# Order of softmax passes, top-k rounds and attention steps in a four-layer gated Flamingo kernel

## The chip, the cores and the metric

The kernel runs on one NeuronCore of a Trainium2 chip. A core has five engines that matter here, each with its own instruction queue: TensorE (PE, matmuls and transposes; its weight loads are listed as PEld), VectorE (DVE), ScalarE (ACT), GpSimd (POOL) and SyncE (SP, which issues most DMAs). They work side by side and wait for each other by semaphores. Matmul results land in PSUM, which this kernel hands out in eight banks of 512 floats a partition; everything else lies in SBUF.

The metric is the device time of one execution in microseconds. Times shown are medians of repeated runs; the profile is of one execution.

## What is computed

`x` is 4 x 256 tokens of 256 features, `ctx` 4 x 256 tokens of 64 features. Four layers follow each other, each with a cross attention and a feed-forward part, both added through a gate:

```python
x = x + jnp.tanh(g_xattn[0]) * _L0_xattn_ref(_layernorm(x), ctx, W_k, b_k, ln_gamma, ln_beta)
x = x + jnp.tanh(g_ffn[0])   * _L0_ffn_ref(_layernorm(x), gate_w, gate_b, expert_w, expert_b)
x = x + jnp.tanh(g_xattn[1]) * _L1_xattn_ref(_layernorm(x), ctx, Wq, Wkv_expand, Wout)
x = x + jnp.tanh(g_ffn[1])   * _L1_ffn_ref(_layernorm(x), w_gate, w_up, w_down)
x = x + jnp.tanh(g_xattn[2]) * _L2_xattn_ref(ctx, _layernorm(x), Wq, Wk, gamma_raw)
x = x + jnp.tanh(g_ffn[2])   * _L2_ffn_ref(_layernorm(x), w12, w3, router_w, expert_bias, sw1, sw2, sw3)
x = x + jnp.tanh(g_xattn[3]) * _L3_xattn_ref(_layernorm(x), ctx, ctx)
x = x + jnp.tanh(g_ffn[3])   * _L3_ffn_ref(_layernorm(x), W_router, W_sgate, Ws_gate_up, Ws_down, We_gate_up, We_down)
```

The change concerns the first third. Of it, the parts that matter:

```python
def _L0_xattn_ref(p, k_v, W_k, b_k, ln_gamma, ln_beta):      # p: the normalised x
    kv = k_v @ W_k.T + b_k
    sim = jnp.einsum('bid,bjd->bij', jnp.einsum('bij,bjd->bid', p, kv), kv) * 256 ** -0.5
    sim = (sim - mean(sim)) * rsqrt(var(sim) + EPS) * ln_gamma + ln_beta
    return softmax(sim)

def _L0_ffn_ref(x, gate_w, gate_b, expert_w, expert_b):      # 8 experts, all computed
    _, top_idx = jax.lax.top_k(x @ gate_w + gate_b, 2)
    all_out = relu(jnp.einsum('nsd,edo->nseo', x, expert_w) + expert_b)
    return jnp.take_along_axis(all_out, top_idx[..., None], axis=2).mean(axis=2)

def _L1_xattn_ref(q, latent_kv, Wq, Wkv_expand, Wout):       # 16 heads of 16, causal
    ...
    attn = softmax(where(tril, q k^T / 4, -max));  out = attn @ v
    return out @ Wout.T

def weight_quant(w):                                         # in L1's feed-forward part
    scale = 1.0 / clip(mean(abs(w)), EPS)
    return clip(round(w * scale), -1, 1) / scale

def _L2_xattn_ref(h, adj_raw, Wq, Wk, gamma_raw):            # a graph over the 256 context tokens
    sim = einsum('bhnd,bhmd->bnm', Q, K) / (4 * 4)
    threshold = top_k(sim, 76)[0][:, :, -1:]
    A = sigmoid(sim) * (sim >= threshold)
    A = (A + swapaxes(A)) * 0.5
    gamma = sigmoid(gamma_raw)
    return (1 - gamma) * adj_raw + gamma * A                 # adj_raw: the normalised x
```

The graph of layer 2 and the ternary weights of layer 1 depend on the context and the weights alone. The kernel therefore computes them early, in gaps of the layers before.

## The kernel before

The 1024 tokens are eight tiles of 128 partitions (two halves of four tiles). The stretch that the change touches is written in one function and ends when the attention of layer 1 ends, at about 258 us of the span. It has three stages.

**Prologue** (to about 54 us). `layernorm(h)` (L169 to L188) normalises the four tiles of a half: statistics on DVE (L176, L177), `ln_ve` (L179), a power on POOL (L181, `ln_rstd`), then four scalings to `xn` on DVE (L185). `transposed` (L190) turns four tiles by PE and copies the result out of PSUM to `xnT` by `evac`, which alternates between DVE (L109) and ACT (L111). Layer 0's attention then goes half by half: `similarities` (L616) turns the tiles, multiplies by the values (L623), copies `oT` on ACT (L628), forms the similarities twice, raw and scaled by gamma (L633), and squares the first on ACT (L641). `softmax0` (L647) computes the variance term on DVE (`s0_ve`, L650), its power on POOL (L652), the scaled similarities and maxima on DVE, and the exponentials on ACT (L666). `add0` (L671) adds the result to `x`. In between stand the key side (`kvmean` L609, `keys` L613 and L614) and the graph's projections and scores (`graph_projections` L462, `graph_scores` L472, copied into `gsim`). A bias block at L447 to L456 splits the expert biases into three bf16 parts on DVE and sends them through DRAM into `eb`, by SP.

**Dense stage** (to about 122 us). `route` (L206) and `choose` (L737) pick two of eight experts for each token. `dense` (L748) computes all eight for a tile: a bias matmul from `eb` (L752), 16 matmuls (L758) into four banks, relus with the chosen weights as scale on ACT (L766), pair sums on POOL (L771, L772). Tiles 0 to 5 run in a loop (L783 to L811), which also holds:

- *rounds of the graph's top-76*. Eight tiles need ten rounds each, 80 in all. A round is a MAX8 (L490) and a MATCH_REPLACE8 (L493) on a row of 256; the tenth has a comparison (L497) instead of the replacement. `graph_rows(n)` issues the next n rounds. The loop asks for 3 + (2, 3, 4, 4, 1, 2)[t], 34 in all.
- `keys1` and `values1` for layer 1 (L527, L542), and the second half's `transposed` and `route`.
- *ternary weights*: `ternary_mean(n)` takes the sum of magnitudes on ACT (two passes, L561), reduces it over partitions on PE (L565) and forms scale and reciprocal on DVE (L567 to L569); `ternary_scale` scales on ACT (L573) and clips on DVE (L574); `ternary_round` finishes on ACT (L578).

**Attention of layer 1** (to about 258 us). `Maxima(b)` (L843) projects the queries of batch b (L204); its `score(j)` makes masked scores of four heads (masks L837, scores L863 and L868) only to find row maxima on DVE (L874, four reductions, then `cm` L879 and L880); `late(j)` turns these (L886) and adds them to the queries on DVE (L889). `Sums(b)` scores again with the maxima subtracted (L903, L908), exponentiates on ACT (L914), multiplies by the values (L922, L927) and divides on DVE (L946, L948). A loop of 24 steps and five more (L978 to L1017) runs them: step n takes head group j = n % 4 of batch n // 4, with the sums one batch behind the maxima. Steps 0 and 1 also hold dense tiles 6 and 7, step 2 the third ternary weight. Each step ends with a call for three rounds.

What sets the order: inside `in_order` a queue keeps the order of the code. PE is in hand order throughout. ACT and DVE are in hand order up to the end of the dense loop, where `all_orders.close()` ends it; from there a scheduler may move their instructions among each other. POOL and SP are always left to the scheduler; the order that it finds is fixed in the built program.

Of the kernel before, what the change touches and what calls it, by code (L numbers as in the profile page):

```python
# [65 lines left out]
def flamingo(ctx: ExitStack, tc: tile.TileContext, a: dict, out: bass.AP):  # L66
# [97 lines left out]
    nc.gpsimd.memset(ones, 1.0)  # L164
    neghalf = const.tile([P, HT], F32, tag="neghalf", name="neghalf")
# [281 lines left out]
    eb_parts = tc.dram_tile([3, E * D], BF16, name="eb_parts")  # L447
    for n in range(3):
        eb_n = const.tile([16, P], BF16, tag=f"eb_{n}", name=f"eb_{n}")
        nc.vector.tensor_copy(eb_n, ebias)  # L450
        if n < 2:
            nc.vector.tensor_sub(ebias, ebias, eb_n)
        nc.sync.dma_start(eb_parts[n].rearrange("(p f) -> p f", p=16), eb_n)
    eb = const.tile([P, 2 * D], BF16, tag="eb", name="eb")
    for j in range(E // 2):
        nc.sync.dma_start(eb[32 * j : 32 * j + 3, :], eb_parts[:, j * 2 * D : (j + 1) * 2 * D])  # L456

# [98 lines left out]
    def ternary_mean(n):  # L558
        wsum = sm([2], "w_sum")
        for j in range(2):  # L560
            nc.scalar.activation(  # L561
                wq1[n][:, j * FF1 : (j + 1) * FF1], raw[n][j], AF.Abs, accum_out=wsum[:, j : j + 1]
            )
        pw = bank()[:, :2]
        nc.tensor.matmul(pw, ones, wsum, start=True, stop=True)  # L565
        m, r = mw[:, n : n + 1], rmw[:, n : n + 1]
        nc.vector.tensor_reduce(m, pw, AX.X, ALU.add)  # L567
        nc.vector.tensor_scalar(m, m, 1.0 / (FF1 * D), 1e-5, ALU.mult, ALU.max)
        nc.vector.reciprocal(r, m)  # L569
# [6 lines left out]
    def ternary_round(n):  # L576
        for j, w in enumerate(raw[n]):
            nc.scalar.activation(wq1[n][:, j * FF1 : (j + 1) * FF1], w, AF.Copy, bias=-ROUND)  # L578

# [7 lines left out]
    with tc.tile_pool(name="l0a", bufs=1) as lp:  # L587
# [15 lines left out]
        for i in range(2):  # L603
            nc.vector.tensor_tensor(
                kvn[:, :, i], pn[i].rearrange("p (h j) c -> p h j c", h=2),
                bk[:, :C].unsqueeze(1).unsqueeze(1).to_broadcast([P, 2, 2, C]), ALU.add,
            )
        mean = lp.tile([P, 2], F32, tag="kvmean", name="kvmean")
# [7 lines left out]
        def similarities(h, tiles):  # L616


            xt = transposed(tiles)
# [8 lines left out]
            nc.scalar.copy(oT, po)  # L628
            sims = [[bank().rearrange("p (i s) -> p i s", i=2) for _ in range(2)] for _ in range(2)]
# [15 lines left out]
            return sims[1], square  # L645

        def softmax0(h, pss, square):  # L647

# [3 lines left out]
            nc.gpsimd.tensor_tensor(rstd, ve, neghalf, ALU.pow)  # L652
            nc.vector.tensor_scalar_mul(rstd, rstd, 1.0 / 16.0)
# [3 lines left out]
            for i in range(HT):  # L657
# [3 lines left out]
                if i % 2:  # L661
# [3 lines left out]
                    for k in (i - 1, i):  # L665
                        nc.scalar.activation(  # L666
                            sim[:, k, :], sim[:, k, :], AF.Exp, bias=nmax[:, k : k + 1], accum_out=ssum[:, k : k + 1]
                        )
            return sim, ssum
# [8 lines left out]
        held = similarities(0, tiles0)  # L678
        tiles1 = layernorm(1)
        nc.scalar.activation(gates, gates, AF.Tanh)  # L680
        qkT2 = lp.tile([P, 2, 2, S], F32, tag="qkT2", name="qkT2")
        graph_projections(qkT2)
        weighted = softmax0(0, *held)
        held = similarities(1, tiles1)
# [4 lines left out]
        weighted = softmax0(1, *held)  # L689
        xt0 = transposed(tiles0)  # L690
        add0(1, *weighted)
# [8 lines left out]
    iota = const.tile([P, E], F32, tag="iota", name="iota")  # L700
    nc.gpsimd.iota(iota, [[1, E]], base=0, channel_multiplier=0, allow_small_or_imprecise_dtypes=True)
# [35 lines left out]
    def choose(pl):  # L737

        lg = sm([HT, E], "r_lg")
        nc.vector.tensor_add(lg, pl, rbias[:, 0:1, :].to_broadcast([P, HT, E]))  # L740
        hot = sm([2, HT, E], "top_hot")
        top2(lg, hot)
        both = sm([HT, E], "r_cw")
        nc.vector.tensor_add(both, hot[:, 0], hot[:, 1])
        nc.vector.tensor_scalar_mul(both, both, 0.5)
        return both

# [30 lines left out]
    counts0 = choose(route(xt0, 0, E))  # L778
# [4 lines left out]
    for t in range(NT - 2):  # L783
# [15 lines left out]
        graph_rows((2, 3, 4, 4, 1, 2)[t])  # L799
# [5 lines left out]
        for n in range(2):  # L805
            if t == 1 + 2 * n:
                ternary_mean(n)
            if t == 2 + 2 * n:
                ternary_scale(n)
            if t == 3 + 2 * n:  # L810
                ternary_round(n)  # L811
    all_orders.close()
# [6 lines left out]
    with ExitStack():  # L819
# [158 lines left out]
        with ExitStack():  # L978
# [4 lines left out]
            for n in range(steps + 5):  # L983
# [20 lines left out]
                if sums is not None:  # L1004
# [3 lines left out]
                    if j == 3:  # L1008
                        plan[n + 2][1].append(sums.turn)
                        plan[n + 3][1].append(sums.output)  # L1010
                for todo in plan[n][1]:
                    todo()
                graph_rows(3)
                if j == 1 and b + 1 < B:
                    if b % 2:
                        xt = transposed(layernorm((b + 1) // 2))
                    following = Maxima(b + 1, xt)  # L1017
    until_l1.close()
# [490 lines left out]
```

## Time and profile before

| what | value |
|---|---|
| median of 3 runs | 822.78 us (820.27 to 823.28) |
| profiled execution, its own time | 823.86 us |
| its span | 822.1 us |
| its mean granted PE clock | 0.924 |
| dense stage: rounds start, first projection of layer 1 | 54.21, 121.89 us |
| projections of Maxima(0) and Maxima(2) start | 121.89, 178.38 us |
| maxima of step 6 and of step 15 | 184.42 to 186.3, end at 234.13 us |

The span is the time from the first to the last instruction of the profiled execution; its own time is 1.8 us more. In the timelines, a line has the start, the length, the engine, the line of the code, the operation and its operands; in square brackets stands how long the engine had been idle, and what released it. Lines that follow each other in one queue without a bracket ran back to back. In the table of stretches, each engine has its busy time and, in parentheses, its number of instructions.

### The profile page before, as it was taken

The page shows a single profiled execution, that of the slowest core. Times are in us where ns is not written, and L with a number is a line of the kernel's source. Part 1 is how long each engine was busy: PE and PEld are TensorE (multiplying, and loading weights), DVE is VectorE, ACT ScalarE, POOL GpSimd, SP SyncE. Part 2 cuts the span into 40 slices and gives each one's busy share as a digit, 9 for nine tenths or more (in the row PEclk, how much of TensorE's full clock was granted, in tenths as well). Part 3 has the DMA queues.
Part 4 walks back from the last instruction along what each step waited for, and adds up shares of the span by engine and source line. Part 5 has one row for each costly group of instructions (what it writes and reads, how often), then busy time and mean ns, then how long its engine had stood idle before and what let it go on. Part 6 is the DMA issues. An engine that isn't in the chain of part 4 may idle for free.

```text
span 822.1 us, 11367 instructions
## 1 busy us (share of the span) xinstructions
PE 706.4 (86%) x4115; PEld 428.4 (52%) x4121; DVE 505.3 (61%) x1398; ACT 283.9 (35%) x583; POOL 213.9 (26%) x254
## 2 busy tenths in 40 slices
PE   4588789779997698639999897999999979989996
PEld 2344345456654466535567646654444335547754
DVE  5685689996767799664224345987777435223334
ACT  1543753323334143203113310166555645023320
POOL 3132553100001434110735273000010010733334
PEclk9877999689999899858999998899999998989999
DMA  7700102200000000000359634000000000379933
GB/s 254 258 0 1 35 24 71 63 1 5 18 2 19 1 1 1 0 1 0 109 180 321 229 97 153 26 1 2 1 1 2 1 1 0 120 249 337 329 106 110
DMA packets 32848, 64.35 MB, mean 78 GB/s; under 512 B 5180, under 2 KB 22488, under 8 KB 32536
## 3 DMA queue, kind: packets, MB, share of 16 engines
q0 software_dynamic: 8224, 31.76, 11.7%
q1 hardware_dynamic: 24136, 31.47, 11.6%
q8 instruction: 33, 0.54, 0.3%
q10 hardware_dynamic: 432, 0.39, 0.2%
q14 instruction: 23, 0.19, 0.1%
HBM read 49.31 MB, written 14.30 MB: 77 GB/s over the span
## 4 chain that ended last, share of the span: by engine, by line
PE 53%; DVE 18%; issue 12%; DMA 7%; ACT 5%; POOL 5%; SPq 0%; DVEq 0%; POOLq 0%; ACTq 0%
PE b L204 18%; PE b L758 6%; PE b L397 5%; PE b L1273 4%; PE b L1288 3%; PE b L1242 3%; PE b L1089 3%; DMA d_w<-in_ffn_r_dram,d_of 3%; DVE pad L1249 3%; PE b L345 3%; DVE x L370 2%; POOL rows_in L295 2%; ACT pT L1280 1%; DVE g_work L493 1%; DVE g_m L490 1%
## 5 line engine op out<-in xcount | busy, mean ns | idle before, releaser
L204 PE MATMUL b<-xnT,w 128*128 128x512 f32 (+2 forms) x288 | 121.1, 578 | 8.0 <-DVE m L874 3.3
L1249 DVE TENSOR_REDUCE pad<-b 128x2 f32<-128x512 f32 x128 | 80.9, 684 | 20.7 <-PE b L1273 20.2
L204 PEld LDWEIGHTS b<-xnT,w 128*128 128x128 f32 (+1 forms) x288 | 56.4, 200 | 64.3 <-issue 54.8
L1280 ACT ACTIVATE pT<-b 128x512 f32<-128x512 f32 x128 | 68.7, 598 | 50.7 <-PE b L1273 50.7
L1242 PE MATMUL b<-kT,qT 32*128 32x256 f32 x512 | 71.9, 417 | 3.2 <-DVE pad L1249 3.2
L1273 PE MATMUL b<-qm,kT 32*128 32x512 f32 x256 | 73.6, 649 | 0.0
L310 POOL DMA_INDIRECT d_w<-in_ffn_r_dram,d_of x46 | 43.9, 954 | 111.6 <-PE b L317 63.1
L758 PE MATMUL b<-w,xnT 128*128 128x512 f32 x128 | 64.6, 662 | 0.0
L204 PE MATMUL b<-d_w,d_xT 128*128 128x256 f32 (+1 forms) x184 | 57.8, 438 | 4.8 <-DMA d_w<-in_ffn_r_dram,d_of 3.9
L1242 PEld LDWEIGHTS b<-kT,qT 32*128 32x128 f32 x512 | 41.8, 191 | 33.2 <-DVE pad L1249 10.7
L397 PE MATMUL b<-w,hT 128*128 128x256 f32 x224 | 53.9, 396 | 2.0 <-DVE hT L383 2.0
L181 POOL TENSOR_TENSOR ln_rstd<-ln_ve,neghalf 128x4 f32<-128x4 f32 x16 | 16.3, 1020 | 137.6 <-DVE ln_ve L179 137.6
L382 ACT ACTIVATE sil<-b 128x512 f32<-128x512 f32 (+1 forms) x28 | 16.7, 597 | 100.7 <-PE b L204 100.7
L397 PEld LDWEIGHTS b<-w,hT 128*128 128x128 f32 x224 | 42.3, 195 | 15.0 <-issue 6.9
L383 DVE TENSOR_TENSOR hT<-b,sil 128x512 f32<-128x512 f32 (+1 forms) x28 | 19.3, 689 | 46.0 <-ACT sil L382 46.0
L771 POOL TENSOR_TENSOR re<-re 128x512 f32<-128x512 f32 (+1 forms) x32 | 32.8, 1026 | 44.2 <-ACT re L766 42.9
L758 PEld LDWEIGHTS b<-w,xnT 128*128 128x128 f32 x128 | 26.5, 213 | 33.9 <-issue 33.9
L1089 PE MATMUL b<-had,zT 128*128 128x256 f32 x128 | 34.7, 430 | 10.6 <-ACT hwork L1100 7.2
L914 ACT ACTIVATE pT<-b 128x384 f32<-128x384 f32 x64 | 26.2, 496 | 49.2 <-PE b L908 49.2
L766 ACT ACTIVATE re<-b,r_cw 128x256 f32<-128x256 f32 x64 | 26.9, 471 | 45.6 <-PE b L758 45.6
L362 POOL DMA_INDIRECT d_yt<-rows_out,d_row x32 | 30.9, 966 | 33.4 <-DMA rows_out<-d_y 24.2
L204 PEld LDWEIGHTS b<-d_w,d_xT 128*128 128x128 f32 x184 | 32.5, 196 | 13.3 <-ACT d_xT L111 4.2
(278 smaller groups left out, 1295.0 us busy)
## 6 DMA issues: line engine op xcount, KB each, us to landing
d_x<-rows_in SPq DMA_DIRECT2D x46, 128.0 KB, 4.7
rows_out<-d_y SPq DMA_DIRECT2D x46, 128.0 KB, 4.5
w<-in_ffn_s_dram SPq DMA_DIRECT2D x13, 384.0 KB, 3.6
w<-in_l_w_dram SPq DMA_DIRECT2D x6, 512.0 KB, 6.1
rows_in<-zero SPq DMA_DIRECT2D x1, 2944.0 KB
w<-in_expert_w_dram SPq DMA_DIRECT2D x4, 512.0 KB, 4.5
x<-in_x_dram SPq DMA_DIRECT2D x8, 128.0 KB, 3.8
kT<-in_l_kT_dram SPq DMA_DIRECT2D x1, 1024.0 KB, 4.8
```

What stands on the lines that cost most here:

```text
L204: nc.tensor.matmul(dst, lhs(kc), rhs(kc), start=kc == 0, stop=kc == KC - 1)
L310: nc.gpsimd.indirect_dma_start(out=w, out_offset=None, in_=src, in_offset=self.indices(self.of[:, n : n + 1]))
L362: nc.gpsimd.indirect_dma_start(out=y, out_offset=None, in_=rows_out, in_offset=self.indices(self.at[:, n, t : t + 1]))
L397: nc.tensor.matmul(po, hT[:hs, j, i * P : (i + 1) * P], w[:hs, 4 * hs : 4 * hs + D], start=j == 0, stop=j == len(ws) - 1,)
L758: nc.tensor.matmul(pe, xt[:, kc, i * P : (i + 1) * P], ws0[j][:, kc * 2 * D : (kc + 1) * 2 * D], start=False, stop=kc == KC - 1,)
L766: nc.scalar.activation(re[:, e % 4, :], pe[:, (e % 2) * D : (e % 2 + 1) * D], AF.Relu, scale=counts[:, i, e : e + 1])
L771: nc.gpsimd.tensor_add(re[:, :n, :], re[:, :n, :], re[:, n : 2 * n, :])
L1089: nc.tensor.matmul(pf[:, c // 2, (c % 2) * 2 * P : (c % 2 + 1) * 2 * P], self.zT[:, c0 : c0 + P], had2[:, n].rearrange("p s q -> p (s q)") ...
L1242: nc.tensor.matmul(pn[:, half * S : (half + 1) * S], self.qT[group(k), ah, g0 + half, qt * P : (qt + 1) * P], kT[group(k), ah, self.b * S ...
L1249: nc.vector.tensor_reduce(self.pads[qt][:, ah, g0 : g0 + 2, k, D3], pn.rearrange("p (g s) -> p g s", g=2), AX.X, ALU.max, negate=True,)
L1273: nc.tensor.matmul(pn, kT[group(k), ah, c : c + P], self.qm[group(k), ah, g0 : g0 + 2, :], start=True, stop=True)
L1280: nc.scalar.activation(self.pT[u][:, k, :], pn, AF.Exp, scale=D3**-0.5)
```

## The change

1. *Prologue.* The copies of the first turned tiles stand ahead of `kvmean` and `keys`. `similarities` is split: a new `out_of` makes `oT`, and for the second half it runs inside the first half's softmax, after its second pair. The variance term and its power move from the softmax into `similarities`. Transposes, `route` and `choose` for the first dense half move ahead of `add0(1)`. The bias block moves behind `layernorm(1)`.
2. *Ternary weights.* `ternary_mean` is split into `ternary_sum` (the two passes on ACT) and the rest, and the pieces move to other tiles and steps.
3. *Rounds.* The dense loop asks for 3 + (2, 6, 6, 6, 2, 4)[t], 44 in all; the attention for 5 in each of its first two steps and then 2 a step, up to the 80. They now stand behind the two scores of a step and ahead of `late` and the following projection.
4. *Order.* `all_orders.close()` moves behind the attention loop, so that ACT and DVE keep the order of the code through it. `layernorm(1)` of the attention moves from step 5 to the end of step 3.

```diff
@@
+    iota = const.tile([P, E], F32, tag="iota", name="iota")
+    nc.gpsimd.iota(iota, [[1, E]], base=0, channel_multiplier=0, allow_small_or_imprecise_dtypes=True)
...
@@
-    def ternary_mean(n):
-        wsum = sm([2], "w_sum")
+    wsums = [sm([2], "w_sum") for _ in range(3)]
+
+    def ternary_sum(n):
+        wsum = wsums[n]
         for j in range(2):
             nc.scalar.activation(
                 wq1[n][:, j * FF1 : (j + 1) * FF1], raw[n][j], AF.Abs, accum_out=wsum[:, j : j + 1]
             )
+
+    def ternary_mean(n):
         pw = bank()[:, :2]
-        nc.tensor.matmul(pw, ones, wsum, start=True, stop=True)
+        nc.tensor.matmul(pw, ones, wsums[n], start=True, stop=True)
...
@@
+        xt = transposed(tiles0)
         mean = lp.tile([P, 2], F32, tag="kvmean", name="kvmean")
...
-        def similarities(h, tiles):
-
-
-            xt = transposed(tiles)
+        def out_of(h, xt):
+
             po = bank()[:, :S]
...
             nc.scalar.copy(oT, po)
+            return oT
+
+        def similarities(h, oT):
...
-            return sims[1], square
-
-        def softmax0(h, pss, square):
-
             ve = sm([HT], "s0_ve")
             nc.vector.tensor_scalar(ve, square, 1.0 / (S * 256.0), 1e-6, ALU.mult, ALU.add)
             rstd = sm([HT], "s0_rstd")
             nc.gpsimd.tensor_tensor(rstd, ve, neghalf, ALU.pow)
+            return sims[1], rstd
+
+        def softmax0(pss, rstd, between=lambda: None):
             nc.vector.tensor_scalar_mul(rstd, rstd, 1.0 / 16.0)
...
+                if i == 1:
+                    between()
             return sim, ssum
...
-        held = similarities(0, tiles0)
         tiles1 = layernorm(1)
+        eb_parts = tc.dram_tile([3, E * D], BF16, name="eb_parts")
+        for n in range(3):
...
+            nc.sync.dma_start(eb_parts[n].rearrange("(p f) -> p f", p=16), eb_n)
+        eb = const.tile([P, 2 * D], BF16, tag="eb", name="eb")
...
+        held = similarities(0, out_of(0, xt))
         nc.scalar.activation(gates, gates, AF.Tanh)
+        xt = transposed(tiles1)
         qkT2 = lp.tile([P, 2, 2, S], F32, tag="qkT2", name="qkT2")
+        oT = []
+        weighted = softmax0(*held, lambda: oT.append(out_of(1, xt)))
         graph_projections(qkT2)
-        weighted = softmax0(0, *held)
-        held = similarities(1, tiles1)
+        held = similarities(1, *oT)
         add0(0, *weighted)
         tiles0 = layernorm(0)
         graph_scores(0, qkT2)
         graph_scores(1, qkT2)
-        weighted = softmax0(1, *held)
         xt0 = transposed(tiles0)
+        pl = route(xt0, 0, E)
+        weighted = softmax0(*held)
+        counts0 = choose(pl)
         add0(1, *weighted)
...
@@
-    counts0 = choose(route(xt0, 0, E))
     tiles1 = layernorm(1)
...
-        graph_rows((2, 3, 4, 4, 1, 2)[t])
+        graph_rows((2, 6, 6, 6, 2, 4)[t])
...
-        for n in range(2):
-            if t == 1 + 2 * n:
-                ternary_mean(n)
-            if t == 2 + 2 * n:
-                ternary_scale(n)
-            if t == 3 + 2 * n:
-                ternary_round(n)
-    all_orders.close()
+        for when, piece, n in (
+            (0, ternary_sum, 0), (1, ternary_mean, 0), (1, ternary_scale, 0), (2, ternary_sum, 1),
+            (2, ternary_round, 0), (3, ternary_mean, 1), (3, ternary_scale, 1), (4, ternary_round, 1),
+        ):
+            if t == when:
+                piece(n)
@@
                     in_l0f.close()
+                    ternary_sum(2)
+                elif n == 3:
                     ternary_mean(2)
                     ternary_scale(2)
+                elif n == 4:
                     ternary_round(2)
...
+                graph_rows(5 if n < 2 else 2)
                 for todo in plan[n][1]:
                     todo()
-                graph_rows(3)
+                if n == 3:
+                    tiles = layernorm(1)
                 if j == 1 and b + 1 < B:
                     if b % 2:
-                        xt = transposed(layernorm((b + 1) // 2))
+                        xt = transposed(tiles)
                     following = Maxima(b + 1, xt)
+    all_orders.close()
     until_l1.close()
```

More of the change, by code (lines that the diff above doesn't have):

```diff
@@ L443, in flamingo @@
     graph = const.tile([P, NT, S], F32, tag="graph", name="graph")
[L447 to L456, printed above, removed]
     gsim = kv1.tile([P, NT, S], F32, tag="gsim", name="gsim")
@@ L578, in ternary_round, with choose @@
             nc.scalar.activation(wq1[n][:, j * FF1 : (j + 1) * FF1], w, AF.Copy, bias=-ROUND)
+    def choose(pl):
+        lg = sm([HT, E], "r_lg")
+        nc.vector.tensor_add(lg, pl, rbias[:, 0:1, :].to_broadcast([P, HT, E]))
+        hot = sm([2, HT, E], "top_hot")
+        top2(lg, hot)
+        both = sm([HT, E], "r_cw")
+        nc.vector.tensor_add(both, hot[:, 0], hot[:, 1])
+        nc.vector.tensor_scalar_mul(both, both, 0.5)
+        return both
     all_orders = ExitStack()
@@ L676, in add0 @@
                 add_scaled(h * HT + i, sim[:, i, :], rec[:, i : i + 1])
-        held = similarities(0, tiles0)
         tiles1 = layernorm(1)
+        eb_parts = tc.dram_tile([3, E * D], BF16, name="eb_parts")
+        for n in range(3):
+            eb_n = const.tile([16, P], BF16, tag=f"eb_{n}", name=f"eb_{n}")
+            nc.vector.tensor_copy(eb_n, ebias)
+            if n < 2:
+                nc.vector.tensor_sub(ebias, ebias, eb_n)
+            nc.sync.dma_start(eb_parts[n].rearrange("(p f) -> p f", p=16), eb_n)
+        eb = const.tile([P, 2 * D], BF16, tag="eb", name="eb")
+        for j in range(E // 2):
+            nc.sync.dma_start(eb[32 * j : 32 * j + 3, :], eb_parts[:, j * 2 * D : (j + 1) * 2 * D])
+        held = similarities(0, out_of(0, xt))
         nc.scalar.activation(gates, gates, AF.Tanh)
+        xt = transposed(tiles1)
         qkT2 = lp.tile([P, 2, 2, S], F32, tag="qkT2", name="qkT2")
+        oT = []
+        weighted = softmax0(*held, lambda: oT.append(out_of(1, xt)))
         graph_projections(qkT2)
-        weighted = softmax0(0, *held)
-        held = similarities(1, tiles1)
+        held = similarities(1, *oT)
         add0(0, *weighted)
@@ L699, in flamingo @@
     nc.gpsimd.memset(onesb, 1.0)
-    iota = const.tile([P, E], F32, tag="iota", name="iota")
-    nc.gpsimd.iota(iota, [[1, E]], base=0, channel_multiplier=0, allow_small_or_imprecise_dtypes=True)
     cmask = const.tile([P, 2, 3, P], BF16, tag="cmask", name="cmask")
@@ L735, in flamingo @@
     l0f = in_l0f.enter_context(tc.tile_pool(name="l0f", bufs=2))
[L737 to L746, printed above, removed]
     def dense(i, xt, counts):
```

## The prediction

> **What bounds the kernel now.** First the page's busy table, then busy time by stretch: the dense stage (54.2 to 121.9 us), the first attention steps (to 181.9) and the steps after them (to 234.1).
>
> ```profile
> PE 706.4 (86%) x4115; PEld 428.4 (52%) x4121; DVE 505.3 (61%) x1398; ACT 283.9 (35%) x583; POOL 213.9 (26%) x254
> ```
>
> ```profile
> 54.20:121.90 67.70, 56.35 (x175) 26.09 (x173) 49.92 (x161) 40.12 (x76) 30.08 (x30) 0.90 0.04 13
> 121.90:181.90 60.00, 49.81 (x284) 30.45 (x285) 57.04 (x189) 17.92 (x36) 11.26 (x12) 0.80 0.17 53
> 181.90:234.10 52.20, 49.89 (x636) 34.15 (x637) 38.20 (x114) 17.57 (x43) 1.01 (x1) 1.00 0.03 9
> ```
>
> Columns: stretch, length, busy time of PE, PEld, DVE, ACT, POOL, granted clock. Over the whole span PE leads, but the middle stretch is VectorE's (57.04 of 60.00, clock 0.80) and the third is PE's (49.89 of 52.20, clock 1.00). The same view for the rounds' tile g_m alone gives 31.29, 36.90 and 3.33 us: nearly all 80 rounds are done when the third stretch begins. Then the timelines:
>
> ```profile
> 51.87 1.01 POOL L181 TENSOR_TENSOR ln_rstd<-ln_ve,neghalf 128x4 f32<-128x4 f32 x1 [5.90 <-DVE ln_ve L179]
> 53.93 2.29 POOL L771 TENSOR_TENSOR re<-re 128x512 f32<-128x512 f32 x2 [1.06 <-ACT re L766]
> 57.37 2.07 POOL L771 TENSOR_TENSOR re<-re 128x512 f32<-128x512 f32 x2 [1.14 <-ACT re L766]
> ```
>
> ```profile
> 54.21 0.42 DVE L490 MAX8 g_m<-gsim 128x8 f32<-128x256 f32 x1
> 54.66 0.09 DVE L493 MATCH_VALUE_LOAD g_work<-g_m,gsim 128x8 f32 x1
> 54.74 0.41 DVE L493 MATCH_REPLACE8 g_work<-g_m,gsim 128x256 f32<-128x256 f32 x1
> 55.18 0.43 DVE L490 MAX8 g_m<-g_work 128x8 f32<-128x256 f32 x1
> ...
> 138.29 1.93 DVE L874 TENSOR_REDUCE m<-b 128x3 f32<-128x384 f32 x4
> ```
>
> ```profile
> 77.59 0.38 PE L565 MATMUL b<-w_sum,ones 128*128 128x2 f32 x2 [2.69 <-ACT wq L561]
> 78.23 8.83 PE L758 MATMUL b<-w,xnT 128*128 128x512 f32 x16
> 88.81 7.13 PE L758 MATMUL b<-w,xnT 128*128 128x512 f32 x16
> ...
> 102.00 0.38 PE L565 MATMUL b<-w_sum,ones 128*128 128x2 f32 x2 [4.57 <-ACT wq L561]
> ```
>
> On POOL the layernorm's power runs ahead of the sums of relus. A round costs 54.21 to 55.18, 0.97 us; its tenth, with L497, 0.93; I use 0.955. PE waits twice for ternary sums (2.69 and 4.57), and 16 L758 matmuls behind such a wait take 8.83 instead of 7.13.
>
> **The change, part by part.**
>
> *Prologue.* The first xnT copy (L109) stands at 15.30 behind kvmean, the bias casts (one of which waits 1.39 for its load) and keys. With these behind it, it starts at 10.9, where kvmean starts now; L633 then follows at 14.8 instead of 18.48. For tiles 1, whose copies now stand inside the first softmax, L633 comes at 25.0 instead of 31.34. But s0_ve(1) now stands on DVE ahead of add0(0), and the squares end 4.1 after L633's start (31.34 to 35.44 now): 25.0 + 4.1 = 29.1. So add0(0) starts at 29.2 against 29.26, and layernorm(0) gains nothing: what was saved ahead of it becomes a wait for ACT, and behind that wait stands everything else of DVE.
>
> Its xn end at 36.1 as now; the copies of gsim (1.2) and xnT (0.7) follow to 38.0, where before the second softmax came first and put the xnT copy at 41.87. Route's matmuls, 3.6 to 4.1 long now, take 38.1 to 41.7: dense(0) starts at 41.7 instead of 46.69, **5.0 earlier**. On DVE the softmax's two pairs end at 41.3, choose takes 2.6 and waits a little for route (to 44.7), add0(1) and identb 2.3, the four statistics 2.3: ln_ve of layernorm(1) comes at 49.3 against 51.62, 2.3 earlier.
>
> The bias DMAs on SP (now issued behind layernorm(1), some 6 us later, still 20 ahead of dense(0), which reads eb first) and POOL's iota, moved to its start, I cost at nothing; were eb late, one DMA of the page's small ones, 4 to 6 us.
>
> *POOL.* In the changed program's built order the power of that layernorm stands behind all four pair sums of dense(0); before, ahead of them. dense(0)'s last sums started at 57.37, so now at 57.37 − 5.0 = 52.4; they take 2.07, the power 1.01, and POOL ends at 55.5. The four xn take 1.3: the rounds start at 56.85. Had the power run when ln_ve was there, they would start at 49.3 + (54.21 − 51.62) = 51.9. So this order costs 5.0, and the rounds start 2.65 later than before. xnT(1), hence PE's route ahead of dense(1), waits with them.
>
> [...] No row shows POOL overtaking, but before nothing tempted it. [...]
>
> *Dense stage.* Before, from the rounds' start to the projection of Maxima(0): 121.89 − 54.21 = 67.7, of which DVE is idle 15.2 (5.00 of it before L538 at 74.54). Busy: 52.5. The diff puts 44 rounds here instead of 34: 10 × 0.955 = 9.6, so 62.1. DVE's waits that stay in hand order: keys 1.2, L574 for ACT 1.6, power behind the relu sums 1.3. Sum 66.2; the projection starts at 56.85 + 66.2 = 123.1 against 121.89. The ternary sums move one tile earlier, so PE's 2.69 and 4.57 vanish, with 2 × 1.7 for the slow groups: 10.7 off PE, but DVE ends last, and PE idles about that long ahead of the projection.
>
> [...] Here a wait of 2.69 already cost 1.7 (8.83 against 7.13). [...]
>
> *First attention steps.* The scheduler filled DVE's time before 138.29 with rounds. In hand order reduces(0) stand ahead of their five rounds, so DVE idles through the projection, dense(6) and the scores: they are ready 13.7 after the projection's start (5.4 + 0.4 + 7.1 + 1.3, less overlaps). From there to Maxima(2)'s projection I count six reduces with cm 12.6, 18 rounds 17.2, five late adds 1.75, two means 0.9, qT copies 0.8, ternary 2.0, layernorm 3.45, xnT 0.6: 39.3; waits for scores 1.2, for scale 1.5, for the power 1.15. Sum 13.7 + 43.2 = 56.9; before 178.38 − 121.89 = 56.5. Maxima(2) at 180.0 against 178.38. So the rounds taken away buy nothing here: idle time replaces them. This queue is the price of the hand order: behind the reduces stand rounds, the late add (PE's second scores wait for it) and the qT copies.
>
> *Later steps.* 18 rounds fall into n = 6 to 14, the stretch that was PE's. reduces(6) come 5.0 after the projection, 185.0 (before 184.42). From 184.42 to the end of reduces(15), 234.13, it was 49.7. DVE's work without rounds is 38.20 − 3.33 = 34.9; with 18 × 0.955 it is 52.1, and DVE still waits for each projection and output: 2.3. I take 54.4. Bounds: 49.7 if PE still sets the pace, 63.6 if every idle moment stays (49.7 + 17.2 − 3.3); the low end is nearer, since a step is 4.3 on DVE (reduces 1.95, rounds 1.9, cm and add) and 3.87 or 4.33 on PE. reduces(15) end at 239.4, 5.3 later; what follows is unchanged.
>
> *Sum.* The profiled execution took 823.86 (span 822.1), 1.1 above the median 822.78. Its stretch grows by 5.3, to 829.2; taken to the median, 828.1.
>
> **Rivals.**
>
> *A. No change, 823.* The 5.0 on POOL isn't paid, because relus come sooner or PE's bank order holds dense(0) less, or the rounds interleave with other work at less than 0.955 (before, some pitches are near 0.84: 36 × 0.115 = 4.1). Then 828.1 − 5.0 = 823.1. For: DVE's gaps between dependent rounds. Against: the built order of POOL.
>
> *B. Faster, 807.* PE, not DVE, paces the dense stage: the 5.0 of the earlier dense(0) and 10.7 from the ternary waits all reach the end: 822.8 − 15.7 = 807.1. For: DVE is idle 15.2 there and gets 9.6. Against: it gets them in hand order, after a start 2.65 later. It decides if DVE's own waits there fall by more than the 4.1 I count and the rounds start by 52.
>
> *C. Much slower, 841.* The scores' banks rotate; a bank held by late's transposes is freed by an add that stands behind two rounds. If PE waits for it in each of nine steps, 1.9 for the rounds less 0.44 for the transposes, it is 9 × 1.46 = 13.1 beyond my sum: 841.2. For: before, PE waited 1.75 for that same add:
>
> ```profile
> 169.72 0.27 PE L837 MATMUL b<-cmask,identb 128*128 128x256 bf16 x1 [1.75 <-DVE qT L889]
> ```
>
> Against: from 187.50 on no mask waits for it. It decides once a step passes 5.7.
>
> **How the numbers follow.** The forecast has 0.52, A 0.22, B 0.14, C 0.12. 0.5% is 4.1 us, about what a measurement of this kernel tells from no change. Forecast's own range: 822 (later steps at PE's pace, 4.7 less, and 1.5 off the dense stage) to 837 (later steps at 63.6). Below 819 lie B and little else; above 838 C. Faster is B and 0.02 of A; the same, 818.7 to 826.9, is A's rest and a little of the forecast's low end, 0.22; slower 0.62.
>
> **What would show it.** Right: POOL's power waits for a relu at about 52, rounds start near 57, PE's L565 waits are gone, Maxima(0) starts near 123 behind a PE wait of 8 us or more for DVE's xnT, DVE idles some 13 us before reduces(0), Maxima(2) near 180, g_m some 17 us busy after that, steps of 4.3 to 5. Wrong: the rounds start by 52; Maxima(0) before 119; PE busier than DVE in the dense stage; or steps n = 6 to 14 still at 3.87 and 4.33.

## The result, and the profile after

The changed kernel takes 827.73 us (median of 13 runs, 824.38 to 833.01), the kernel before in the same series 822.54 us (13 runs, 820.27 to 825.91): ratio **1.0072**, 95% interval 1.005 to 1.0094. The change makes the kernel 5 to 6 us slower. Its profiled execution has a span of 827.6 us against 822.1.

The page's busy table of the changed kernel:

```profile
PE 707.5 (85%) x4121; PEld 426.7 (52%) x4121; DVE 510.6 (62%) x1398; ACT 283.3 (34%) x583; POOL 212.2 (26%) x254
```

Nearly the same work, 5.5 us longer: DVE's busy time grows by 5.3 us over the same 1398 instructions, and what changed most is where engines wait. To see that, both executions are cut at marks that both have: the first bias matmul of dense(0) (D0), the first round, the projection of Maxima(0) (M0), the first reduction of step 0 (R0), the projection of Maxima(2) (M2), and the first matmul of layer 1's feed-forward part (FF). Busy time by stretch, columns as in the prediction; first the kernel before, from the first round to M0, M0 to R0, R0 to M2, and M2 to the end of step 15's maxima:

```profile
54.21:121.89 67.68, 56.33 (x175) 26.07 (x173) 49.90 (x161) 40.11 (x76) 30.07 (x30) 0.90 0.04 13
121.89:138.29 16.40, 16.40 (x65) 9.26 (x66) 15.63 (x53) 4.43 (x12) 5.24 (x6) 0.90 0.15 46
138.29:178.38 40.09, 29.90 (x204) 18.17 (x203) 38.04 (x127) 13.12 (x24) 6.02 (x7) 0.74 0.20 59
178.38:234.60 56.22, 53.91 (x656) 37.48 (x656) 42.08 (x126) 18.07 (x45) 1.01 (x1) 1.00 0.03 9
```

The same four stretches of the changed kernel:

```profile
55.32:123.85 68.53, 54.20 (x167) 25.57 (x166) 59.37 (x185) 32.94 (x66) 25.06 (x26) 0.82 0.08 24
123.85:138.94 15.09, 15.09 (x60) 8.94 (x60) 1.24 (x4) 4.09 (x10) 2.37 (x3) 0.82 0.00 1
138.94:182.44 43.50, 30.04 (x213) 17.47 (x209) 38.46 (x117) 15.30 (x28) 8.07 (x9) 0.76 0.18 55
182.44:242.50 60.06, 55.21 (x654) 37.05 (x654) 50.53 (x158) 17.94 (x44) 1.01 (x1) 1.00 0.03 8
```

The third busy time is DVE's. In the dense stage it rises from 49.90 to 59.37. The same view for the rounds' tile g_m alone rises from 31.28 to 39.85: nine more rounds, since in the profile of before the scheduler had already moved a 35th ahead of M0. Another 1.4 us are the four xn ahead of Maxima(0) (below). Between M0 and R0 it falls from 15.63 to 1.24 of 15.09: the hole that the hand order leaves. In the last stretch it rises from 42.08 to 50.53, where PE had set the pace.

Start times of the marks give this table, in us; each column after the first is the distance from the mark before it, and FF to end is what remains of the span:

| kernel | D0 | to first round | to M0 | to R0 | to M2 | to FF | to end |
|---|---|---|---|---|---|---|---|
| before | 46.69 | 7.5 | 67.7 | 16.4 | 40.1 | 82.1 | 561.6 |
| changed | 40.46 | 14.9 | 68.5 | 15.1 | 43.5 | 86.7 | 558.5 |
| difference | −6.2 | +7.3 | +0.9 | −1.3 | +3.4 | +4.6 | −3.2 |

dense(0) does start 6.2 us earlier, but the first round 1.1 us later. POOL's timeline in the changed kernel shows why (start, length, engine, line, operation):

```profile
50.54 2.06 POOL L785 TENSOR_TENSOR re<-re 128x512 f32<-128x512 f32 x2 [0.98 <-ACT re L780]
52.56 1.01 POOL L183 TENSOR_TENSOR ln_rstd<-ln_ve,neghalf 128x4 f32<-128x4 f32 x1
```

and DVE's, at the rounds' start and around M0:

```profile
47.58 1.07 DVE L181 TENSOR_SCALAR ln_ve<-ln_mv 128x4 f32<-128x4 f32 x1
53.61 1.78 DVE L187 TENSOR_SCALAR xn<-x,ln_mv,ln_rstd 128x256 f32<-128x256 f32 x4 [4.96 <-POOL ln_rstd L183]
55.32 0.41 DVE L479 MAX8 g_m<-gsim 128x8 f32<-128x256 f32 x1
...
109.89 4.22 DVE L187 TENSOR_SCALAR xn<-x,ln_mv,ln_rstd 128x256 f32<-128x256 f32 x4 [1.13 <-POOL ln_rstd L183]
...
123.02 0.68 DVE L109 COPY xnT<-b 128x512 f32<-128x512 f32 x1
125.93 0.42 DVE L109 COPY qT<-b 128x256 f32<-128x256 f32 x1 [2.23 <-PE b L206]
129.34 0.42 DVE L109 COPY qT<-b 128x256 f32<-128x256 f32 x1 [2.99 <-PE b L206]
...
138.94 1.95 DVE L885 TENSOR_REDUCE m<-b 128x3 f32<-128x384 f32 x4 [8.78 <-PE b L879]
```

The input of the power is there at 48.65 (its DVE instruction itself took 1.07 us beside a POOL addition, 0.17 in the kernel before), but POOL is still at the pair sums, and DVE waits 4.96. Later DVE is the one that others wait for: the xnT copy ends at 123.7, and PE has been idle 8.36 when it starts the projection, while its waits for the ternary sums are gone:

```profile
74.93 0.38 PE L558 MATMUL b<-w_sum,ones 128*128 128x2 f32 x2
...
93.08 0.38 PE L558 MATMUL b<-w_sum,ones 128*128 128x2 f32 x2
...
123.85 6.37 PE L206 MATMUL b<-xnT,w 128*128 128x256 f32 x16 [8.36 <-DVE xnT L109]
```

Then roles change again: DVE waits 2.23, 2.99 and 8.78, 14.0 us in all, for PE. In the later steps without a projection DVE runs with hardly a gap, 4.3 to 5 us a step (busy 4.16 of 4.30 and 4.82 of 4.99 us between these lines):

```profile
193.04 1.94 DVE L885 TENSOR_REDUCE m<-b 128x3 f32<-128x384 f32 x4
...
197.34 1.94 DVE L885 TENSOR_REDUCE m<-b 128x3 f32<-128x384 f32 x4
...
202.33 1.94 DVE L885 TENSOR_REDUCE m<-b 128x3 f32<-128x384 f32 x4
```

### The profile page after: what moved, and what is told of

Its sections match the earlier page's. It is cut to its first block, busy times and chain, and to the rows that moved or that the text cites. A ratio compares the mean times of both kernels' runs of the same rounds, so it can differ in the third digit from the quotient of the medians.

```text
span 827.6 us, 11378 instructions
## 1 busy us (share of the span) xinstructions
PE 707.5 (85%) x4121; PEld 426.7 (52%) x4121; DVE 510.6 (62%) x1398; ACT 283.3 (34%) x583; POOL 212.2 (26%) x254
## 4 chain that ended last, share of the span: by engine, by line
PE 59%; DVE 19%; issue 10%; DMA 4%; ACT 4%; POOL 3%; SPq 0%; ACTq 0%; DVEq 0%; POOLq 0%
PE b L206 21%; PE b L772 6%; PE b L399 6%; PE b L1290 4%; PE b L1305 3%; PE b L1259 3%; PE b L347 3%; PE b L1106 3%; DVE pad L1266 3%; DMA d_w<-in_ffn_r_dram,d_of 2%; DVE xn L187 2%; POOL ln_rstd L183 2%; DVE x L372 2%; DVE g_work L482 1%; ACT pT L1297 1%
## 5 line engine op out<-in xcount | busy, mean ns | idle before, releaser
L772 PE MATMUL b<-w,xnT 128*128 128x512 f32 x128 | 59.9, 623 | 0.0
L199 PE MATMUL b<-ident,xn 128*128 128x128 f32 x80 | 17.4, 359 | 29.1 <-DVE xn L187 28.0
L187 DVE TENSOR_SCALAR xn<-x,ln_mv,ln_rstd 128x256 f32<-128x256 f32 x64 | 26.5, 468 | 24.5 <-POOL ln_rstd L183 24.5
L885 DVE TENSOR_REDUCE m<-b 128x3 f32<-128x384 f32 x64 | 31.1, 547 | 13.9 <-PE b L879 13.9
## 6 DMA issues: line engine op xcount, KB each, us to landing
rows_in<-zero SPq DMA_DIRECT2D x1, 2944.0 KB, 14.3
```

The source lines that it names most:

```text
L187: nc.vector.tensor_scalar(xn, x[h * HT + i], mv[:, i, 0:1], rstd[:, i : i + 1], ALU.subtract, ALU.mult)
L772: nc.tensor.matmul(pe, xt[:, kc, i * P : (i + 1) * P], ws0[j][:, kc * 2 * D : (kc + 1) * 2 * D], start=False, stop=kc == KC - 1,)
```

## The experiments

The runs were made on two other chips, where the kernel before took 833.98 to 835.62 us; nearly all of the 11 to 13 us more lie behind FF (there it has 573.1 us from FF to the end instead of 561.6). So ratios are compared, each to the kernel before in the same series, and stages with the changed kernel's own repetition. All stages side by side, from one execution each:

| kernel | ratio (95%) | D0 | to round | to M0 | to R0 | to M2 | to FF | to end |
|---|---|---|---|---|---|---|---|---|
| before again | | 47.26 | 7.5 | 68.6 | 16.4 | 40.1 | 82.1 | 573.1 |
| changed again | 1.006 (1.0038 to 1.0082) | 40.04 | 15.9 | 68.5 | 13.9 | 43.5 | 86.0 | 571.2 |
| power first | 1.0032 (1.0006 to 1.0058) | 42.12 | 12.2 | 68.5 | 13.8 | 43.5 | 86.0 | 569.3 |
| no sums of tile 0 | 1.002 (0.9995 to 1.0044) | 40.51 | 9.7 | 70.2 | 14.2 | 43.5 | 88.1 | 566.8 |
| rounds in the hole | 0.998 (0.9957 to 1.0002) | 42.20 | 15.7 | 60.5 | 14.4 | 43.5 | 86.8 | 571.1 |
| attention scheduled | 0.9989 (0.9963 to 1.0015) | 40.12 | 15.5 | 65.6 | 17.2 | 39.7 | 82.8 | 571.3 |
| rounds late | 1.0093 (1.0067 to 1.0119) | 40.95 | 15.2 | 68.5 | 15.3 | 43.5 | 86.4 | 572.9 |
| before, early sums | 0.994 (0.9912 to 0.9968) | 47.48 | 7.5 | 63.2 | 16.4 | 40.7 | 83.7 | 573.0 |
| before, new prologue | 0.9961 (0.9938 to 0.9984) | 41.91 | 12.1 | 66.7 | 16.4 | 40.1 | 82.1 | 570.9 |
| best, scheduled | 0.9926 (0.9904 to 0.9948) | 40.39 | 11.1 | 63.7 | 17.6 | 39.4 | 82.6 | 571.1 |
| best, by hand | 0.986 (0.9836 to 0.9883) | 41.51 | 12.1 | 60.5 | 14.3 | 38.1 | 84.6 | 574.0 |
| by hand, fuller hole | 0.9861 (0.9831 to 0.9892) | 40.27 | 12.6 | 61.8 | 14.7 | 38.2 | 82.8 | 573.5 |

D0 of the versions with the new prologue varies by 2 us between executions, with the time that PE's matmuls took there: the graph's projections took 3.67 and 3.68 us in runs 1 and 3 (D0 at 42.12 and 42.20) and 1.93 in run 2 and in the repetition of the changed kernel (40.51 and 40.04), while the first scaling xn started between 7.55 and 8.24 us in all of them. In the profile of the changed kernel they took 2.40, from 22.50 us on, with the clock granted to PE at 0.50 from 20.1 to 23.4 us and at 1.00 behind; in that of the kernel before 1.93, at 1.00.

**1. Power first.** POOL in hand order from layernorm(1) to dense(0):

```diff
+    pool_order = ExitStack()
+    pool_order.enter_context(in_order(mybir.EngineType.Pool))
     tiles1 = layernorm(1)
...
         means[t] = dense(t % HT, *((xt0, counts0) if t < HT else (xt1, counts1)))
         if t == 0:
+            pool_order.close()
```

> The changed kernel with one thing undone: on POOL the power of layernorm(1) stands ahead of dense(0)'s pair sums again. Theory (queue order on POOL costs 5 us): in the changed kernel DVE waits 4.96 us for that power, and DVE sets the dense stage's end, so the rounds start at 50.3 instead of 55.3, the projection of Maxima(0) at 118.9 instead of 123.85, and the whole is 5 us faster than the changed kernel: 822.7, no different from the kernel before. Rival (the wait is covered): another wait of the dense stage takes its place, PE or the ternary chain on ACT, and the projection of Maxima(0) moves by less than 1.5 us: 826 to 828.

The ratio falls from 1.006 or 1.0072 to 1.0032, some 2.3 to 3.3 us, between the two expectations; the intervals overlap, so the stages carry the reading. D0 to the first round takes 12.2 us instead of 14.9 and 15.9, so 2.7 to 3.7 were won, not 5.0; all later stages stay up to FF, so nothing takes the gain back there. The other runs agree: with the power first this stage takes 11.1 to 12.6 us (runs 7 to 10), without it 15.2 to 15.7 (runs 3 to 5). Where the rest went, DVE's and POOL's timelines of this run show:

```profile
50.54 3.85 DVE L187 TENSOR_SCALAR xn<-x,ln_mv,ln_rstd 128x256 f32<-128x256 f32 x4 [1.12 <-POOL ln_rstd L183]
54.30 0.42 DVE L479 MAX8 g_m<-gsim 128x8 f32<-128x256 f32 x1
```

```profile
49.50 1.01 POOL L183 TENSOR_TENSOR ln_rstd<-ln_ve,neghalf 128x4 f32<-128x4 f32 x1 [1.85 <-DVE ln_ve L181]
50.47 2.07 POOL L785 TENSOR_TENSOR re<-re 128x512 f32<-128x512 f32 x2
52.97 2.08 POOL L785 TENSOR_TENSOR re<-re 128x512 f32<-128x512 f32 x2 [0.43 <-ACT re L780]
```

The power now runs at once, but the four xn take 3.85 while POOL makes the pair sums that the power waited for in the changed kernel. In the kernel before, the same four took 1.38 here, ahead of POOL's sums, and 2.80 ahead of Maxima(0), where POOL's addition of 109.59 to 111.67 ran beside them:

```profile
52.91 1.38 DVE L185 TENSOR_SCALAR xn<-x,ln_mv,ln_rstd 128x256 f32<-128x256 f32 x4 [1.12 <-POOL ln_rstd L181]
...
109.65 2.80 DVE L185 TENSOR_SCALAR xn<-x,ln_mv,ln_rstd 128x256 f32<-128x256 f32 x4 [1.14 <-POOL ln_rstd L181]
```

**2. No sums of tile 0.** To test whether POOL's work is what slows xn, the same kernel without those sums; tile 0 then adds one expert's share only:

```diff
-            if j % 2:
+            if j % 2 and summed:
                 for n in (2, 1):
                     nc.gpsimd.tensor_add(re[:, :n, :], re[:, :n, :], re[:, n : 2 * n, :])
-        nc.gpsimd.tensor_add(means[0][:, 0, :], means[0][:, 0, :], means[1][:, 0, :])
+        if summed:
+            nc.gpsimd.tensor_add(means[0][:, 0, :], means[0][:, 0, :], means[1][:, 0, :])
```

> The kernel with the power first, but without the pair sums of dense(0) on POOL: tile 0 then adds one expert's share instead of the sum. Theory (DVE's four xn are held up by POOL working at the same time): xn takes 1.4 us instead of 3.85 and the rounds start 2.4 us earlier after dense(0)'s start: 9.7 us instead of 12.2. Rival (xn is slow for another reason, such as PE's transposes or DMA writes): xn stays above 3 us and the rounds at 12.

As the theory said, to the tenth. DVE's timeline of this run:

```profile
48.93 1.38 DVE L187 TENSOR_SCALAR xn<-x,ln_mv,ln_rstd 128x256 f32<-128x256 f32 x4 [1.12 <-POOL ln_rstd L183]
50.23 0.42 DVE L479 MAX8 g_m<-gsim 128x8 f32<-128x256 f32 x1
```

So of the changed kernel's way from D0 to the first round, 2.7 to 3.7 us are the queue order, and another 2.5 are DVE held up by POOL, which the order had hidden. The remaining 9.7 us are still 2.2 more than in the kernel before. Of the 2.5 us only 0.9 reach M0 in run 2 (D0 to M0 takes 79.9 us against 80.7 in run 1): DVE then waits 2.95 us for PE at the keys of layer 1 where it waited 1.36.

**3. Rounds in the hole.** Nine rounds move from the end of the dense loop into step 0:

```diff
-        graph_rows(3)
+        graph_rows(3 if t < 5 else 0)
...
-        graph_rows((2, 6, 6, 6, 2, 4)[t])
+        graph_rows((2, 6, 6, 6, 0, 0)[t])
...
             xt = transposed(tiles)
+            graph_rows(4)
             mx, sums, following = Maxima(0, xt), None, None
...
                     add_mean(5 + n)
+                    graph_rows((5, 0)[n])
```

> The changed kernel with nine rounds moved: those that stand behind the last layernorm of the dense loop go behind the copies for Maxima(0), four ahead of its query copies and five ahead of the reduces of step 0. Theory (hand order leaves a hole): PE waits 8.36 us for xnT behind these rounds and DVE then idles 14.0 us until the reduces of step 0, so the projection starts at 115.4 instead of 123.85, the hole shrinks to about 5 us, and all that follows comes 8.4 us earlier: 819.3. Rival (DVE is the bound from there to Maxima(2) whatever stands where): the reduces of step 0 start no earlier than 137 and the time stays at 826 to 828.

The theory holds: rounds to M0 60.5 us instead of 68.5, the stages behind it as in the changed kernel and its repetition, ratio 0.998, which is 0.8 to 0.9% or about 7 us below the changed kernel. PE waits 0.30 us ahead of the projection instead of 8.36, and of DVE's wait of 8.78 ahead of step 0's maxima 4.05 is left:

```profile
118.38 5.71 PE L206 MATMUL b<-xnT,w 128*128 128x256 f32 x16 [0.30 <-DVE xnT L109]
```

```profile
132.79 1.95 DVE L885 TENSOR_REDUCE m<-b 128x3 f32<-128x384 f32 x4 [4.05 <-PE b L879]
```

**4. Attention scheduled.** The change's fourth part undone:

```diff
             if t == when:
                 piece(n)
+    all_orders.close()
...
-    all_orders.close()
     until_l1.close()
```

> The changed kernel, but ACT and DVE are in hand order only to the end of the dense loop, as before; the scheduler then puts 13 of the rounds ahead of the reduces of step 0 and nearly all others ahead of Maxima(2). Theory (hand order is what costs): projection of Maxima(0) unchanged at 123.9, Maxima(2) at 171 to 174 instead of 182.4 since 36 rounds instead of 46 are left for this stretch, later steps at 3.87 and 4.33 us again: 816 to 818, 5 us below the kernel before. Rival (the hand order is neutral and the loss lies in the dense stage): 826 to 828.

The ratio falls to 0.9989, by 0.7 to 0.8%, so this hand order costs some 6 to 7 us; the rival is out. (Runs 3 and 4 both fill the hole, so their gains don't add.) But I had expected 5 us below the kernel before, and it is 1 us: M2 lies at 178.0, not at 171 to 174. Two stretches give 3.8 and 3.2 to 3.9 back (R0 to M2, M2 to FF), and rounds to M0 gives 2.9, since the scheduler let the xnT copy pass three rounds; M0 to R0 takes 17.2 instead of 15.1 or 13.9. The hole is filled: DVE is busy 14.24 of 17.17 us from M0 to R0:

```profile
121.22:138.39 17.17, 17.17 (x65) 9.90 (x66) 14.24 (x49) 4.09 (x10) 4.26 (x5) 0.84 0.01 1
138.39:178.04 39.65, 26.88 (x205) 16.03 (x204) 38.11 (x127) 13.24 (x24) 6.33 (x7) 0.87 0.21 60
```

It put all the rounds left ahead of the later steps (none is behind 182 us), so the stretch from R0 to M2 stays DVE's, 38.11 of 39.65 busy: the rounds in it take 19.91 us by the view for g_m, 19.64 in the kernel before. That was the step of my expectation that failed: I took rounds off that stretch which the scheduler then brought forward from later ones.

**5. Rounds late.** The 18 rounds of steps 6 to 14 go to steps 15 to 20:

```diff
-                graph_rows(5 if n < 2 else 2)
+                graph_rows(5 if n < 2 else 2 if n < 6 else 0 if n < 15 else 3)
```

> The changed kernel with the 18 rounds of steps 6 to 14 moved to steps 15 to 20, three a step; nothing else. Theory (those rounds make DVE set the pace of steps that were PE's): from the projection of Maxima(2) to the first matmul of layer 1's feed-forward it takes 82 to 83 us instead of 86.7, as in the kernel before (82.1), and the ratio to the kernel before falls from 1.0072 to about 1.002. Rival (DVE is short of time in steps 15 to 20 too, so that the work only moves): that stretch stays above 85.5 us and the ratio at 1.006 or more.

The rival is right about the end: 86.4 us from M2 to FF, ratio 1.0093 (its interval overlaps the changed kernel's). The theory is right about the steps themselves: from M2 to the start of step 15's maxima it is 53.5 us (236.98 − 183.44) against 58.2 in the changed kernel (240.59 − 182.44) and 54.3 before (232.65 − 178.38). Of the 4.6 us won there 4.3 are lost between step 15 and FF, 32.9 us instead of 28.6. PE's waits there (what waited for what, us in total, times, longest) name the divisions by the softmax sums (att), the longer of which stands behind rounds on DVE:

```profile
PE b L970 <- DVE att L959: 3.7, 2, 3.2
```

In the changed kernel DVE is busy 17.81 of the 28.61 us between step 15 and FF; with the 18 rounds it is 31.15 of 32.92. So there is free time behind step 15, but not enough for 18 rounds, which take 16.2 us by the view for g_m.

**6. The kernel before with early sums.** `ternary_mean` split and its pieces moved as in the change, nothing else:

```diff
-            if t == 1 + 2 * n:
-                ternary_mean(n)
...
+        for when, piece, n in (
+            (0, ternary_sum, 0), (1, ternary_mean, 0), (1, ternary_scale, 0), (2, ternary_sum, 1),
...
```

> The kernel before with one part of the change alone: the sums of magnitudes on ACT stand a tile ahead of the matmul that reads them. Theory (PE's two waits are on the path as long as DVE has idle time): 2.69 and 4.57 us vanish with 1.7 us each for the slow groups behind them, DVE's idle 15.2 us of the dense stage falls by about as much, and the projection of Maxima(0) starts at 112 to 115 instead of 121.9: 813 to 816. Rival (DVE in hand order sets the dense stage's end): less than 3 us is gained: 820 to 823.

Ratio 0.994, 5 us: between the two. PE's two waits are gone, rounds to M0 fall from 67.7 or 68.6 to 63.2, and then DVE ends last: its xnT copy ends at 118.06, and PE has waited 7.05 us (the profile names no releaser here).

```profile
117.39 0.67 DVE L109 COPY xnT<-b 128x512 f32<-128x512 f32 x1
```

```profile
118.16 1.19 PE L204 MATMUL b<-xnT,w 128*128 128x256 f32 x2 [7.05 <-issue]
```

**7. The kernel before with the new prologue**, and the power first as in run 1:

```diff
+        xt = transposed(tiles0)
         mean = lp.tile([P, 2], F32, tag="kvmean", name="kvmean")
...
+        pl = route(xt0, 0, E)
+        weighted = softmax0(*held)
+        counts0 = choose(pl)
         add0(1, *weighted)
```

> The kernel before with the new prologue alone, the power of layernorm(1) held ahead of dense(0)'s pair sums. Theory (the 6 us by which dense(0) starts earlier are mostly a wait later): dense(0) starts 6 us earlier than before, but the rounds only 1.5 us, since choose and add0(1) are little earlier and the four xn run beside POOL's pair sums (3.85 us instead of 1.38): ratio 0.996 to 0.999. Rival (PE sets the pace in this kernel's dense stage, as its waits for ACT suggest, and ACT gains the 6 us as well): the projection of Maxima(0) comes 5 to 6 us earlier: ratio 0.992 to 0.994.

Ratio 0.9961, as the theory said: of some 5 us at D0, 4.6 are lost until the first round. The interval (0.9938 to 0.9984) just reaches the rival's 0.994, but the projection of Maxima(0) comes 1.2 to 2.6 us earlier (120.72 against 121.89 and 123.36), not the rival's 5 to 6.

**8. and 9. Versions that put the parts together.** Both have the power first and 35 rounds in the dense loop. One ends the hand order with the dense loop and asks for three rounds a step; the other keeps it, has nine rounds in the hole as in run 3, and then:

```diff
-                graph_rows(5 if n < 2 else 2)
+                graph_rows((4, 3, 1, 1, 1, 1, 1, 1, 1, 1, 1, 1, 1, 1, 1)[n] if n < 15 else 2)
```

> The changed kernel with three things: power of layernorm(1) ahead of dense(0)'s pair sums, no rounds asked for behind the last layernorm of the dense loop (35 rounds there), and hand order of ACT and DVE ended with that loop, so that the scheduler fills the hole ahead of step 0's reduces. Theory (the three costs add up: 2.7 us at the rounds' start, 8 ahead of Maxima(0), 4 in the later steps): against the kernel before 6 us earlier at dense(0), 4.7 lost until the rounds, 10 gained to Maxima(0): ratio 0.986 to 0.990. Rival (with 45 rounds the stretch from Maxima(0) to Maxima(2) becomes DVE's and takes back what the dense stage gives): ratio 0.994 or more.

> The changed kernel, hand order kept through the attention: power of layernorm(1) first, nine rounds ahead of step 0's reduces as in the run with rounds in the hole, then 4, 3 and one a step to step 14, two a step from 15 to 22. Theory (hand order is no loss if the rounds stand where DVE has nothing else): to Maxima(0) as in the previous run, from step 0's reduces to Maxima(2) 36 to 38 us instead of 43.5, later steps 83 instead of 86.7: ratio 0.983 to 0.987. Rival (one round a step still delays the late add, and two a step delay the graph): ratio 0.990 or more.

Scheduled: 0.9926, a gain, between theory and rival: 63.7 us to M0 instead of the 58 expected. In its trace 42 maxima of rounds stand ahead of the xnT copy (41 in run 4), though the code asks for 35. By hand: **0.986**, as the theory said, the fastest with the next, 1.4% below the kernel before and 2% below the changed one. DVE is busy 8.96 of 14.32 us in the former hole, R0 to M2 takes 38.1, and one round a step costs nothing: M2 to step 15's maxima takes 53.8 us, as before (54.3). M2 to FF takes 84.6, more than the 83 expected.

```profile
114.11:128.43 14.32, 14.32 (x60) 8.40 (x60) 8.96 (x29) 4.42 (x11) 2.36 (x3) 0.86 0.01 2
```

**10. Fuller hole.** Four more rounds ahead of step 0's maxima, four fewer from step 15 on:

```diff
-                    graph_rows((5, 0)[n])
+                    graph_rows((9, 0)[n])
```

> The version by hand with four more rounds in the hole ahead of step 0's reduces (13 in all) and four fewer from step 15 on. Theory (DVE still idles 4 us there, and late rounds are paid in full): reduces of step 0 at most 0.5 us later, feed-forward of layer 1 3 us earlier: ratio 0.981 to 0.984. Rival (the copies of the queries stand behind these rounds, or the late ones were free): ratio 0.986 or more.

0.9861: no gain that can be told. M2 to FF is 1.8 us shorter, but rounds to M0, which the edit doesn't touch, 1.3 longer. Inconclusive.

**11. and 12. Both kernels again**, unchanged.

> The changed kernel as it is, so that the other runs can be read beside it on their chip. If what is known of it holds: ratio 1.007, dense(0) to the rounds 15 us, rounds to Maxima(0) 68.5, Maxima(2) to layer 1's feed-forward 86.7. One thing is open: behind that the changed kernel took 558.5 us against 561.6 in the two profiles. If that is the change's doing, it is again 3 us shorter here than in the kernel before on this chip; if it is one execution's chance, the two are within 1.5 us.

> The kernel before as it is, for its stages on this chip: dense(0) to the rounds 7.5 us, rounds to Maxima(0) 67.7, Maxima(2) to layer 1's feed-forward 82.1. From there to the end within 1.5 us of the changed kernel's on this chip if the 3.1 us were chance, 3 us more if they were not.

The stages come again within 1.2 us; the largest differences are D0 to the first round (15.9 instead of 14.9) and M0 to R0 (13.9 instead of 15.1) of the changed kernel. From FF to the end it is 2.0 us less in the changed kernel, between the two bounds, from one execution each. Over all twelve runs that stretch scatters from 566.8 to 574.0 without order. So whether 2 to 3 us behind FF are the change's doing stays open.

## Why the prediction was right

828.1 was predicted, 5.3 us above the kernel before; 827.73 was measured, 5.2 above it. The likeliest case is the one that happened, by the mechanism named. That the two agree within half a microsecond is luck: terms of the sum were off by up to 2.3 us, and 3.2 us behind FF, which no term held, brought the total back. Point by point:

- *dense(0) earlier*: 5.0 predicted, 6.2 (7.2 in the repetition) measured. The wait of s_ve(1) for the squares is there, 3.05 us, but ends 1.1 earlier than reckoned. The bias loads, costed at nothing, were in time: the first bias matmul follows route's matmuls without a wait.
- *POOL's order*: right that the power waits for the pair sums, that DVE then idles (4.96 measured, 5.0 predicted) and that the first round comes later than before (55.32; 56.85 predicted, 54.21 before). **Wrong in size**: "this order costs 5.0". Undone, it gives 2.7 to 3.7 at the rounds' start and 0.3 to 0.4% in all (run 1), because the xn then run beside the sums and take 3.85 instead of 1.38 (run 2). The sum used 1.3 for them on either side. Rival A, priced with the same 5.0, was too large too; its condition, that the order isn't paid, fell.
- *dense stage*: 66.2 predicted, 68.5 measured, with 44 rounds in it. Three terms were mis-sized. DVE's waits are 5.7 instead of 4.1, since its clips of the ternary weights (L567) wait 3.2 for ACT and not 1.6. The four xn for Maxima(0) ran beside 4.14 us of POOL's additions and took 4.22, while the 2.80 of the kernel before were in the sum's 52.5. And the rounds added 8.6 by the view for g_m, not 9.6. That PE's two waits would vanish and PE then idle ahead of the projection was right (8.36), and run 6 shows why it brings nothing: alone it gives 5 us, after which DVE ends last, and the change adds 8.6 us of rounds to DVE.
- *the hole*: 13.7 predicted, 15.1 and 13.9 measured, with 14.0 us of DVE's idle time. Run 3 fills it with rounds that stood ahead of the xnT copy and gains 8 us in its stage, the largest that a single run took out of one stage. R0 to M2: 43.2 predicted, 43.5 measured.
- *later steps*: from M2 to the end of step 15's maxima 5.0 + 54.4 = 59.4 predicted, 60.1 measured. (The end of step 15's maxima in the kernel before is 234.6, not 234.13: the four reductions from 232.65 take 1.94. By its own terms the sum's 5.3 should have been 4.8.) Run 5 takes the rounds out and M2 to the start of step 15's maxima falls from 58.2 to 53.5; without hand order (run 4) it is 55.0, and 54.3 before.
- *"what follows is unchanged"*: between step 15 and FF +0.7, behind FF −3.2 in the profile, −2.0 in the repetition. This hid that the stretch to FF had grown by 8.7, not 5.3. Without it the measured time would have been some 2 to 3 us above the forecast, still inside its range.
- *rivals*: B fell, DVE is busy 59.37 of 68.53 in the dense stage and PE waits for it. C fell, from M2 on the masks wait for the maxima (four times, 0.18 to 2.01 us) and once for attT (1.05), none for a late add.

So the gains that the change aims at are there: 6.2 us ahead of dense(0), and early sums that are worth 5 us in the kernel before (run 6). The first is given back until the rounds start: 2.7 to 3.7 to POOL's queue, 2.5 to POOL's additions beside xn, 2.2 because DVE's own work ahead of the power moved up less than dense(0) did (ln_ve starts at 47.58 instead of 51.62). The second is given back to the added rounds; the hand order then leaves a hole and puts the other rounds where they cost. The moves of the bias block and of layernorm(1) to step 3 were not run alone.

## What to carry to other kernels

Work that fills gaps is worth as much as the place it stands in: the changed kernel, with its rounds where the change puts them, costs 0.7%, and the version by hand, with the same 80 rounds elsewhere in a hand order, saves 1.4% (run 1 puts 0.3 to 0.4% of that down to POOL's power put first). The table of busy time by stage and engine points to such places, though run 10 shows that a place with idle time left need not pay. Before fixing an order by hand, look at what the engine will wait for at each point, and put filling work ahead of that wait, not behind it. When one engine is made to start earlier, look on the queues of all others, also those left to a scheduler, for what now arrives together.

## What the runs showed of the hardware

POOL's additions slowed DVE's scalings. Four scalings of 128 x 256 floats on DVE took 1.38 us with POOL idle, 1.78 beside one addition of 0.72 us, 2.80 beside additions of 2.08, 3.85 where two pairs of additions of 2.07 and 2.08 overlap them in part (run 1), and 4.22 beside 4.14 us of additions; without the additions they were back at 1.38 (run 2). POOL's additions were hardly longer for it: a pair took 2.07 us with no xn beside it (57.37 in the profile of before) and 2.07 or 2.08 beside xn (50.47 in run 1, 109.59 in the profile of before); that of 53.93 there, which began beside the last xn, took 2.29. But one on POOL that began with a longer scaling of DVE in the kernel before (90.17, beside L574 at 90.18) took 1.28 instead of 0.73. The maxima of the rounds were not slowed: the one at 55.18 in the profile of before, beside POOL's additions of 53.93 to 56.22, took 0.43 us like the others. So the price in this kernel was 0.4 to 2.8 us for four scalings, more the longer POOL added beside them.

The clock granted to PE, and not the last wait, told how slow the next matmuls were. The projection of Maxima(0) took 6.37 us behind 8.36 us of idle time in the changed kernel, 5.08 behind 8.37 in run 1, and 5.71 behind only 0.30 in run 3; that of Maxima(2), at a clock of 1.00, took 3.69. In the changed kernel the clock stood at 0.50 when the projection of Maxima(0) began: PE had waited 3.07 us for xn ahead of the transposes and had then worked in short pieces, and at the transposes, at 112.2 us, the clock fell from 1.00. It was back at 1.00 at 129.3 us, 5.4 us after the projection's start. Runs 1 and 3 have the same wait, 3.08 us, and the same short pieces; that the clock was low there too is my estimate, from their 5.08 and 5.71 us against 3.69. In the kernel before, the clock was 0.50 from 79 to 82 us, behind the wait of 2.69, and from 103 to 106 us, behind the wait of 4.57, and the 16 matmuls took 8.83 and 8.78 us instead of the 7.13 at a clock of 1.00. So behind the shorter wait they took 1.70 us longer, as much as behind the longer one, 1.65.
